# Graph attention kernel: a node group's x_l and x_r are loaded and bent four rounds ahead of its states

## The chip, the core and the metric

The kernel runs on one core of one Trainium2 chip. The metric is the device time of one execution in microseconds, compared as medians of runs of the two kernels on the same chip. Beside the times there is one profiled execution of the kernel, recorded instruction by instruction.

In a core, five sequencers run independently and meet at semaphores. TensorE (PE; its weight loads are listed as PEld) multiplies into PSUM. VectorE (DVE) and ScalarE (ACT) do elementwise work and reductions. GpSimd (POOL) issues the indirect gathers here. SyncE (SP) issues nearly all other DMAs, one after the other, in program order: a DMA whose condition isn't met holds up every DMA behind it.

## The reference

One layer of graph attention (GATv2, 8 heads of 16 channels) and a feed-forward block over 12,500 nodes and 400,000 edges that are sorted by destination:

```python
h  = relu(layernorm(x))
x_l, x_r = ln(h) @ W_l, ln(h) @ W_r                  # 12500 x 128
e  = edge_attr @ W_e                                 # self edges: the mean of edge_attr
m  = leaky_relu(x_l[src] + x_r[dst] + e, 0.2)
alpha = (m * att).sum(per head)
a  = softmax of alpha over the edges of each dst
out = segment_sum(x_l[src] * a, dst) + bias
h  = h + out
result = x + h + gelu(ln(h) @ W1 + b1) @ W2 + b2
```

Every node has a self edge, whose source and destination are the node itself.

## The kernel before

**Preparation.** The first part norms x, writes the x_l rows (136 floats: 128 and eight ones) to DRAM as `xl_dram`, and keeps h in SBUF (`h_sb`). x_r follows as three bf16 parts (`xs_dram`).

**Edges.** `window_edges` runs over 782 pairs of 256 edges, called c. It is a pipeline by hand: in round r, stage (late, f) of the table `stages` works on pair c = r - late. `gather` (-4) fetches the x_l rows of the pair's 512 edges with four indirect DMAs of 128 rows on GpSimd; in 24 pairs the rows are loaded from `late_dram` by SP in their place. `combine` (0) sums x_l, x_r and e in PSUM, `slope` and `bend` (1) make the leaky ReLU, `score` (2), `lowest` (3) and `weigh` (3) give the scores, their least and the exponents, `turn` (4), `keep_turned` (5) and `collect` (6) multiply by the gathered rows, `own_heads` (7) keeps what belongs to each head in the tile `rec`, and `put` (8) writes two records by SP to one of two DRAM tensors `state[0]` and `state[1]`, alternately. The buffer for gathered rows has 12 slots, so the gather of pair c needs the collecting of pair c - 12 to be done.

**Node groups.** The 98 tiles of 128 nodes are finished in 25 groups of 4 (the first has 2). A group has a round d["round"], from which the states of its nodes are complete in DRAM; groups are at least GAP = 23 rounds apart, and the last is at round 790, after the last `put` (round 789). The table `steps` gives each step's round after that: `f_load` (0) has SP load both states (`st`), x_l (`f_xl`) and x_r (`f_xr`), in this order; `f_order` (1, ACT) puts x_l in head order; `f_z` (2, PE) adds x_l and x_r; `f_bend` (3, ACT and DVE) makes the leaky ReLU of the self edges; `f_score` (4, PE) gives their scores; `f_low` (5, DVE) takes the least over both states and the self edge; then come `f_exp`, `f_den`, `f_out`, `f_h`, the second norm, the two products, gelu and `f_store` (19), which ends with SP's DMA of the output. The second gelu stands in its own table `early` at 17, which a round runs ahead of `stages`.

**What sets the order.** Everything here is scheduled by hand (`tc.manual_schedule`), so each engine's order is the order of this loop (L1320):

```python
for r in range(-AHEAD, max(last_round, groups[-1]["round"] + 20)):
    in_round(r, early)
    ...                          # stages: the edge pairs
    in_round(r, steps)           # the node groups
    ...                          # x_r of later nodes, late rows
    ...                          # late_stages: windows(r + 3), put(r - 8)
```

In a round SP therefore meets the loads of `steps` before the round's `put`. The states are read only when every earlier `put` to them has landed, and a later `put` waits for the load to be done. PSUM has two banks called acc, shared by `collect` and, through `bank_of`, by the group steps.

Of the kernel before, what the change touches and what calls it, by code (L numbers as in the profile page):

```python
# [47 lines left out]
AHEAD = 4  # L48
# [49 lines left out]
def node_groups(nt):  # L98

    first = nt % GN  # L100
    return ([(0, first)] if first else []) + [(t, GN) for t in range(first, nt, GN)]
# [6 lines left out]
def done_after(nt, n_edges):  # L108

    return [-(-(t + n) * P * edges_per_node(nt, n_edges) // U) + SPARE for t, n in node_groups(nt)]  # L110
# [24 lines left out]
def tile_gnn(  # L135
# [612 lines left out]
    with tc.If(fast == 1) as cmp:  # L748
        window_edges(
            tc, n_edges, ea_t, NT, NE, NUE, ident, ident_b, wer, we_z, negrep, diag, nid, farw, bias_r, b2_r, w1_sb, w2_sb,  # L750
            cols, xl_dram, xl_t, xs_dram, xs_t, dc_dram, du_dram, late_dram, state, clear, xr_steps, qs, raw_steps, raw, x_t, out_t, h_sb, src_sb, first_sb,
        )
# [74 lines left out]
def window_edges(  # L827
# [30 lines left out]
    with ExitStack() as es:  # L858
# [9 lines left out]
        NL = next(n for n in range(1, EQ + 1) if EQ % n == 0 and EQ // n <= 1024)  # L868
# [180 lines left out]
        groups = [{"t0": t, "n": n, "ts": slice(t, t + n)} for t, n in node_groups(NT)]  # L1049
# [5 lines left out]
        def bank_of(d, name, ring="acc"):  # L1055
            d[name] = ps2.tile([P, EPR], F32, name=ring)
            return d[name]

        def f_load(d):
            n, ts = d["n"], d["ts"]  # L1060
            d["st"] = fin.tile([P, 2, GN, SW], F32, name="st", tag="big", bufs=3)
            for i in range(2):
                nc.sync.dma_start(d["st"][:, i, 0:n], state[i].rearrange("(t p h) f -> p t (h f)", p=P, h=H)[:, ts, :])
            d["xl"] = fin.tile([P, GN, XW], F32, name="f_xl")
            nc.sync.dma_start(d["xl"][:, 0:n], xl_t[:, ts, :])
            d["xr"] = fin.tile([P, GN, NS, P], BF16, name="f_xr")
            nc.sync.dma_start(d["xr"][:, 0:n], xs_t[:, ts, :, :])
# [137 lines left out]
        def f_up(k):  # L1205
            def up(d):
                n, u = d["n"], bank_of(d, f"u{k}")
                nc.tensor.matmul(  # L1208
                    u[:, 0 : n * P],
                    w1_sb[:, k * P : (k + 1) * P],  # L1210
                    d["hT"][:, 0:n].rearrange("p t f -> p (t f)"),
                    start=True,
                    stop=True,
                )

            return up

        def f_gelu(k):
            def gelu(d):
                n = d["n"]  # L1220
                if k == 0:
                    d["gel"] = fin.tile([P, 2, GN * P], F32, name="gel", tag="big", bufs=3)
                nc.scalar.activation(
                    d["gel"][:, k, 0 : n * P], d[f"u{k}"][:, 0 : n * P], AF.Gelu, bias=cols[:, 5 + k : 6 + k]
                )

            return gelu
# [13 lines left out]
        def f_store(d):  # L1241
# [29 lines left out]
            (3, mean),  # L1271
        )
        SUM_STEP = 2
        early = ((17, f_gelu(1)),)
        steps = (
            (0, f_load),
            (1, f_order),
            (2, f_z),
            (3, f_bend),
            (4, f_score),  # L1280
            (5, f_low),
            (6, f_exp),
            (7, f_den),
            (8, f_out),
            (9, f_h),
            (10, f_stats),
            (11, f_root),
            (12, f_scale),
            (13, f_turn),
            (14, f_turned),  # L1290
            (15, f_up(0)),
            (16, f_up(1)),
            (16, f_gelu(0)),
            (18, f_down),
            (19, f_store),
        )
        GAP = 23
        last_round = n_pr + LATE + 2
        free = SUM_STEP * (NL - 1) + 5
        for d, u in zip(groups, done_after(NT, n_edges)):  # L1300
            d["round"] = max(free, (u // UP if u < NUE else n_pr) + LATE + 2)
            free = d["round"] + GAP

        def in_round(r, table, groups=groups):
            for k, f in table:
                for d in groups:
                    if d["round"] + k == r:
                        f(d)
# [8 lines left out]

        CLEAR = 8
        with tc.manual_schedule():
            for r in range(-AHEAD, max(last_round, groups[-1]["round"] + 20)):  # L1320
                in_round(r, early)
                for late, f in stages:
                    c = r - late
                    if 0 <= c < n_pr:
                        f(c)
                for late, f in sum_stages:
                    i, off = divmod(r - late, SUM_STEP)
                    if off == 0 and 0 <= i < NL:
                        f(i)
                if r > 0 and r % CLEAR == 0 and r // CLEAR < NT // GT:  # L1330
                    clear(r // CLEAR)
                in_round(r, steps)
                in_round(r, enumerate(xr_steps), qs[1:])
                in_round(r, enumerate(raw_steps), raw)
                for late, f in late_stages:
                    c = r - late
                    if 0 <= c < n_pr:
                        f(c)
# [358 lines left out]
```

## Time and profile before

| | |
|---|---|
| median of 3 runs | 4050.42 us (4048.72 to 4051.7) |
| the profiled execution's own time | 4055.89 us |
| its span, first to last instruction | 4053.7 us |
| mean granted TensorE clock | 0.955 |
| busy: PE / POOL / DVE / ACT | 3555.2 / 2984.9 / 2539.5 / 2135.2 us |
| chain of waits: PE / POOL / DMA / issue | 40% / 24% / 22% / 13% of the span |

The page of the profile has several views that are used below. The groups of instructions give, for each line, the count, the mean duration and the idle time of the engine ahead of them with its releaser. The view of one line gives its shortest, median and longest duration and its first and last start. The chain of waits follows the work that ended last back through what released each step. The timeline lists instructions in order of time; for SP it shows the issue of DMAs, not their landing.

The stages of the span in the profile: preparation until about 186 us, the edge pairs with the node groups among them from the first gather (186.4 us) until the last `own_heads` (ends at 4005.7 us), and the last node group alone, until 4053.7 us.

### The profile page before, as it was taken

How to read it: one execution, taken by the hardware profiler on the slowest of the kernel's cores; microseconds unless marked ns; L12 is line 12 of the kernel's file. 1: busy time of each engine (PE TensorE's matmuls, PEld its weight loads, DVE VectorE, ACT ScalarE, POOL GpSimd, SP SyncE). 2: the span in 40 equal slices, each digit the busy share in tenths (PEclk: the TensorE clock that was granted, in tenths of full speed). 3: DMA queues.
4: the chain of work that ended last, by engine and by line, in shares of the span. 5: the costliest groups of instructions: out<-in, count | busy, mean ns of one | idle time of the engine just before them, and what ended most of it. 6: DMA issues, size and time to landing. Idle time of an engine off the chain costs nothing.

```text
span 4053.7 us, 65778 instructions
## 1 busy us (share of the span) xinstructions
PE 3555.2 (88%) x19254; PEld 2501.5 (62%) x19255; DVE 2539.5 (63%) x5834; ACT 2135.2 (53%) x4638; POOL 2984.9 (74%) x3156
## 2 busy tenths in 40 slices
PE   2388888998989999999999999999989999989986
PEld 2356665665666666666666666666766666666664
DVE  5656665766666666666666666666666665666654
ACT  4544444544445555565455556555555555545543
POOL 4777777777777777777777777777777777777772
PEclk6699999999999999999999999999999999999998
DMA  5668878777766666656665665656666666565562
GB/s 160 198 165 198 185 194 197 171 163 165 172 124 126 126 124 131 123 121 129 132 125 124 128 129 120 136 123 117 124 136 126 124 130 128 107 135 114 120 134 50
DMA packets 648212, 560.85 MB, mean 138 GB/s; under 512 B 386387, under 2 KB 525506, under 8 KB 647602
## 3 DMA queue, kind: packets, MB, share of 16 engines
q1 hardware_dynamic: 547266, 339.01, 33.7%
q0 software_dynamic: 100000, 217.41, 30.2%
q8 instruction: 156, 2.56, 0.3%
q14 instruction: 214, 1.75, 0.2%
q10 hardware_dynamic: 576, 0.13, 0.0%
HBM read 489.81 MB, written 66.32 MB: 137 GB/s over the span
## 4 chain that ended last, share of the span: by engine, by line
PE 40%; POOL 24%; DMA 22%; issue 13%; SPq 1%; DVE 0%; ACT 0%; POOLq 0%; DVEq 0%; ACTq 0%
POOL xs L896 22%; DMA xs<-xl_dram,src_sb 21%; PE z L942 9%; PE acc L1000 8%; PE ab L960 7%; PE pt_ps L986 4%; PE z L938 4%; PE z L941 2%; PE ab L959 2%; POOL raw L270 2%; PE acc L1233 1%; PE acc L1208 1%; DMA lu<-in_dst 1%; SPq L282 0%; DMA state<-rec 0%
## 5 line engine op out<-in xcount | busy, mean ns | idle before, releaser
L896 POOL DMA_INDIRECT xs<-xl_dram,src_sb x3029 | 2873.0, 949 | 923.2 <-issue 796.0
L978 ACT ACTIVATE p<-ab,rec 128x256 f32<-128x256 f32 x1563 | 656.8, 472 | 1056.5 <-DVE rec L967 1044.3
L1009 DVE TENSOR_TENSOR own<-acc,diag 128x272 f32<-128x272 f32 x782 | 344.1, 440 | 1068.5 <-PE acc L1000 1039.6
L938 PE MATMUL z<-ident,xs 128*128 128x128 f32 x3125 | 573.3, 283 | 353.0 <-DMA xs<-xl_dram,src_sb 318.3
L938 PEld LDWEIGHTS z<-ident,xs 128*128 128x128 f32 x3125 | 399.5, 142 | 772.3 <-DMA xs<-xl_dram,src_sb 434.5
L1000 PE MATMUL acc<-xs,pt 128*128 128x136 f32 x6250 | 874.9, 284 | 0.2 <-DVE f_yo L1247 0.2
L942 PE MATMUL z<-ea,we_z 128*128 128x512 f32 x1564 | 835.4, 617 | 0.0
L1000 PEld LDWEIGHTS acc<-xs,pt 128*128 128x128 f32 x6250 | 802.6, 195 | 0.4 <-PE pt_ps L986 0.4
L960 PE MATMUL ab<-m,negrep 128*128 128x512 f32 x1564 | 801.4, 594 | 0.0
L991 ACT COPY pt<-pt_ps 128x512 f32<-128x512 f32 x782 | 455.9, 583 | 623.3 <-PE pt_ps L986 611.5
L986 PEld LDWEIGHTS pt_ps<-ident,p 128*128 128x128 f32 x3125 | 407.8, 146 | 438.2 <-issue 386.4
L967 DVE TENSOR_REDUCE rec<-ab 128x2 f32<-128x512 f32 x781 | 540.2, 692 | 123.4 <-PE ab L960 113.2
L953 DVE TENSOR_TENSOR m<-z,zs 128x512 f32<-128x512 f32 x782 | 533.0, 682 | 115.0 <-ACT zs L948 114.7
L948 ACT ACTIVATE zs<-z 128x512 f32<-128x512 f32 x782 | 472.2, 604 | 41.4 <-DMA dlw<-dc_dram 33.6
L986 PE MATMUL pt_ps<-ident,p 128*128 128x128 f32 x3125 | 489.2, 281 | 2.2 <-ACT pt L991 1.3
L1015 DVE TENSOR_REDUCE rec<-own 128x34 f32<-128x272 f32 x782 | 340.9, 436 | 26.7
L942 PEld LDWEIGHTS z<-ea,we_z 128*128 128x128 f32 x1564 | 306.5, 196 | 32.5
L960 PEld LDWEIGHTS ab<-m,negrep 128*128 128x128 f32 x1564 | 300.6, 192 | 37.1 <-issue 1.2
L941 PE MATMUL z<-ne,xrw 128*128 128x512 bf16 x782 | 304.0, 389 | 0.2 <-DMA xs<-xl_dram,src_sb 0.2
L959 PE MATMUL ab<-ne,farw 128*128 128x512 bf16 x782 | 299.6, 383 | 0.0
L924 DVE TENSOR_SCALAR ne<-dlw,nid 112x512 bf16<-112x512 bf16 x782 | 289.8, 371 | 13.0 <-DMA dlw<-du_dram 13.0
L270 POOL DMA_INDIRECT raw<-in_x,src_raw x96 | 95.5, 995 | 71.3 <-DMA raw_dram<-raw 40.1
(198 smaller groups left out, 2235.6 us busy)
## 6 DMA issues: line engine op xcount, KB each, us to landing
dlw<-dc_dram SPq DMA_DIRECT2D x196, 384.0 KB
ea<-in_ea_t SPq DMA_DIRECT2D x196, 256.0 KB
ea_s<-in_ea_t SPq DMA_DIRECT2D x98, 512.0 KB
xs<-xl_dram,src_sb POOLq DMA_INDIRECT x3029
state<-rec SPq DMA_DIRECT2D x1563, 9.0 KB
xrw<-xs_dram SPq DMA_DIRECT2D x782, 24.0 KB
state<-empty SPq DMA_DIRECT2D x28, 504.0 KB
st<-state SPq DMA_DIRECT2D x48, 288.0 KB
```

The lines of the kernel that those rows point to most:

```text
L896: nc.gpsimd.indirect_dma_start(out=xs[:, j, :], out_offset=None, in_=xl_dram, in_offset=bass.IndirectOffsetOnAxis(ap=src_sb[:, c * KP + j ...
L938: nc.tensor.matmul(z[:, j * P : (j + 1) * P], d["xs"][:, j, 0:P], ident, start=(j == 0), stop=False, is_transpose=True)
L941: nc.tensor.matmul(z[:, :e], xrw[c % NV], d["ne"][:, :e], start=False, stop=False)
L942: nc.tensor.matmul(z[:, :e], we_z[:, c % QP, :], d["ea"][:, :e], start=False, stop=True)
L948: nc.scalar.activation(d["zs"][:, :e], d["z"][:, :e], AF.Copy, scale=SLOPE)
L953: nc.vector.tensor_tensor(d["m"][:, :e], d["z"][:, :e], d["zs"][:, :e], op=OP.max)
L960: nc.tensor.matmul(ab[:, :e], negrep.rearrange("p n h -> p (n h)"), d["m"][:, :e], start=False, stop=True)
L967: nc.vector.tensor_reduce(d["rec"][:, :, CX], d["ab"].rearrange("p (u e) -> p u e", e=U), AX.X, OP.min)
L978: nc.scalar.activation(d["p"][:, us], d["ab"][:, us], AF.Exp, bias=d["rec"][:, i, CX:SH], scale=-1.0)
L986: nc.tensor.transpose(d["pt_ps"][:, js], d["p"][:, js], ident)
L991: nc.scalar.copy(d["pt"][:, :e], d["pt_ps"][:, :e])
L1000: nc.tensor.matmul(d["acc"][:, i, :], d["pt"][:, j * P : (j + 1) * P], d["xs"][:, j, :], start=(j == js[0]), stop=(j == js[-1]),)
```

## The change

`f_load` is cut in two. A new step `f_state` loads the two states; `f_load` keeps x_l and x_r. In the table, `f_load`, `f_order`, `f_z` and `f_bend` go to rounds -4, -3, -2 and -1, `f_state` takes round 0, and `f_score` and all that follow come three rounds earlier than they were (4 to 1, and so on to 19 to 16; the early gelu from 17 to 14). The first group may start at round 201 where it was 199; the loop's end follows the last step.

```diff
-        def f_load(d):
+        def f_state(d):
             n, ts = d["n"], d["ts"]
             d["st"] = fin.tile([P, 2, GN, SW], F32, name="st", tag="big", bufs=3)
             for i in range(2):
                 nc.sync.dma_start(d["st"][:, i, 0:n], state[i].rearrange("(t p h) f -> p t (h f)", p=P, h=H)[:, ts, :])
+
+        def f_load(d):
+            n, ts = d["n"], d["ts"]
             d["xl"] = fin.tile([P, GN, XW], F32, name="f_xl")
             nc.sync.dma_start(d["xl"][:, 0:n], xl_t[:, ts, :])
             d["xr"] = fin.tile([P, GN, NS, P], BF16, name="f_xr")
...
-        early = ((17, f_gelu(1)),)
+        early = ((14, f_gelu(1)),)
         steps = (
-            (0, f_load),
-            (1, f_order),
-            (2, f_z),
-            (3, f_bend),
-            (4, f_score),
-            (5, f_low),
...
-            (19, f_store),
+            (-4, f_load),
+            (-3, f_order),
+            (-2, f_z),
+            (-1, f_bend),
+            (0, f_state),
+            (1, f_score),
+            (2, f_low),
...
+            (16, f_store),
         )
         GAP = 23
         last_round = n_pr + LATE + 2
-        free = SUM_STEP * (NL - 1) + 5
+        free = SUM_STEP * (NL - 1) + 7
...
-            for r in range(-AHEAD, max(last_round, groups[-1]["round"] + 20)):
+            for r in range(-AHEAD, max(last_round, groups[-1]["round"] + 17)):
```

No instruction and no DMA is added or removed.

More of the change, by code (lines that the diff above doesn't have):

```diff
@@ L1273, in window_edges @@
         SUM_STEP = 2
-        early = ((17, f_gelu(1)),)
+        early = ((14, f_gelu(1)),)
         steps = (
-            (0, f_load),
-            (1, f_order),
-            (2, f_z),
-            (3, f_bend),
-            (4, f_score),
-            (5, f_low),
[L1282 to L1294, printed above, removed]
-            (19, f_store),
+            (-4, f_load),
[5 more added lines that the diff above has]
+            (2, f_low),
+            (3, f_exp),
+            (4, f_den),
+            (5, f_out),
+            (6, f_h),
+            (7, f_stats),
+            (8, f_root),
+            (9, f_scale),
+            (10, f_turn),
+            (11, f_turned),
+            (12, f_up(0)),
+            (13, f_up(1)),
+            (13, f_gelu(0)),
+            (15, f_down),
+            (16, f_store),
         )
```

## The prediction

> **What bounds the kernel now.** The first view is the page's groups of instructions, where the gather on GpSimd is the costliest, and then the view of that line.
>
> ```profile
> L896 POOL DMA_INDIRECT xs<-xl_dram,src_sb x3029 | 2873.0, 949 | 923.2 <-issue 796.0
> L896 POOL DMA_INDIRECT xs<-xl_dram,src_sb x3029: 940/945/1702, 186.4 to 3981.5; - x190
> ```
>
> Read the first and last start: 3029 gathers start between 186.38 and 3981.53 us, so one each 1.2533 us (3795.2 / 3028): 0.95 busy and 0.30 of issue, from first to last. The idle time is almost all "issue", so GpSimd's own sequence makes it. No gather waits for a buffer: if I pair the gather of c with the collecting of c - 12, whose slot it takes, GpSimd comes 17.7 us later than that in the median and 8.3 us in the nearest case (c = 109). TensorE idles for the gathered rows (434.5 us ahead of its weight loads in the views of waits). So until 3982.5 us, when the last gather ends, the clock is GpSimd's. Work of the other engines costs nothing there unless they fall back by over 8.3 us.
>
> The Trainium skill (Perfetto Trace Analysis, "Identifying the Most-Contended Engine") takes occupancy as the measure for GpSimd, and by it the bound would be TensorE: 88% against GpSimd's 74%. Then each stall that the new order gives or takes on TensorE in the 24 groups would count in full, about 24 us for one microsecond per group. The row says that GpSimd has no free time in its 74%, since the rest is issue. I take the row: the sum over the middle is zero.
>
> What follows the last gather is 71 us, and there the chain of waits, in order of time, decides:
>
> ```profile
> 3999.84 0.69 DVE f_yo L1247
> 4001.15 1.95 DMA state<-rec
> 4003.12 3.00 DMA state<-rec
> 4006.24 1.42 DMA state<-rec
> 4007.78 1.41 DMA state<-rec
> 4009.31 1.42 DMA state<-rec
> 4010.84 1.45 DMA state<-rec
> 4012.78 2.00 DMA state<-rec
> 4015.24 0.50 SPq L1063
> 4015.79 4.96 DMA f_xl<-xl_dram
> 4020.89 1.08 PE acc L1081 x4
> 4021.99 1.48 PE acc L1086 x12
> 4023.49 0.70 ACT f_zs L1095
> 4024.21 0.76 DVE f_m L1097
> 4025.02 1.89 PE acc L1103 x8
> ```
>
> Columns: start, length, what. Group 23 (round 764) stores at round 783. SP waits there for f_yo until 4000.5 us, and the last 13 puts stand behind it. They then go one pair per landing, 1.53 us apart, although their records were ready by 4005.7. The last lands at 4014.78; only then are the states loaded, and behind them x_l, which lands after 4.96 us, then z, its bend and the scores. Timeline rows of the same stretch:
>
> ```profile
> 4000.56 0.39 SPq L1248 DMA_DIRECT2D out<-f_yo  x1
> 4001.15 11.96 SPq L1022 DMA_DIRECT2D state<-rec  x13
> 4014.79 0.95 SPq L1063 DMA_DIRECT2D st<-state  x2
> 4026.93 0.19 DVE L1114 TENSOR_TENSOR f_mn<-f_mn,acc 128x32 f32<-128x32 f32 x1 [1.85 <-PE acc L1103]
> ```
>
> From the states' issue at 4014.79 (call it T) to the first minimum that needs states and scores, 12.14 us pass; from there to the span's end 26.77 us.
>
> **The change, part by part.**
>
> *x_l, x_r, order, z and bend out of the last group's chain.* Its `f_load` goes to round 786, `f_z` to 788, right behind the last collecting (787); they lie beside the last puts. Loads at about 4002.2 (below), landed by 4007 or so; z 2.6 us, f_zs 0.7, f_m 0.8, scores 1.9 by the rows above: 4013 to 4014, while the states can't have landed. So the chain is T, states landed, two minima. The states' landing isn't on the page. From above, x_l lands at T + 5.96 with both states ahead of it; from below, the earliest put in the middle that follows two state loads issues 3.41 us after the first. In one group its second put waits, and the row shows it:
>
> ```profile
> 1275.26 0.95 SPq L1063 DMA_DIRECT2D st<-state  x2
> 1278.76 1.88 SPq L1022 DMA_DIRECT2D state<-rec  x2
> ```
>
> A pair of puts takes 0.9 us undisturbed, so this second one came at 1280.3, 5.0 us after the first load's issue. I take T + 4.9, plus one minimum (0.20) and gaps: the second minimum at T + 5.15. **Gain 7.0 us (5.9 to 8.4).** Nothing replaces it as last: the scores are about 3 us early.
>
> *Later steps three rounds earlier.* Group 23's `f_store` moves from round 783 to 780. TensorE is busy without a break from 3951.5 on, and the steps that pass round 780 were already behind that point, so its work up to the last collecting is the same: one f_up (0.86) and f_down (1.8) come ahead of pair 780, 2.6 us, and are missing behind it. What goes are stalls in the shortened last rounds (0.66 us for the gelu on ACT, 0.2 to 0.4 for f_yo). I work the last rounds out with the row durations (round 3.95; turning 0.44, collecting 0.93, score 1.14): the last `own_heads` ends near 4004.1, and c = 777 is ready at 3999.8. SP now has its wait for f_yo near 3990.7, and its puts, a pair each 1.5 us against rounds of 2.5 to 4, have caught up at 777, issued at 4000.8.
>
> *What SP's queue gets in exchange.* Round 786 puts x_l and x_r, 272 + 384 KB, ahead of the last four puts (778 to 781). The Trainium skill (DMA: Bandwidth & Descriptors, "Queues, rings and completion order") speaks against this: each DMA engine consumes a ring's descriptors in order, so the puts get behind 656 KB; at that page's 435 GB/s ceiling an estimated 1.5 us. The rows give more: behind the output's 256 KB the second pair took 3.00 us, not 1.42. By size this is 1.58 x 656 / 256 = 4.0 us extra; nothing is the other end. With the page T would be about 4011.6, with the full 4.0 near 4014. I take 2.6 us extra, between, since the loads are issued ahead of the first such pair and part of them has gone before it. So: loads at 4001.7 and 4002.3, put 778 at 4003.0, landed 4007.0; 779 at 4008.5, 780 at 4010.1, 781 issued 4010.6 and landed 4012.6. **T = 4012.6, gain 2.2 us (0.3 to 4.6).** The low end is T = 4014.5, the high one T = 4010.2, without any delay.
>
> *The cover of the state load shrinks.* `f_low` stood five rounds behind it and now stands two. On DVE the queue behind a late `f_low` is the next round's `own_heads`, `lowest` and `bend`, for which TensorE waits, and then the gathers' slots. Two rounds after the load stands `f_z` in the trace of before; it begins 9.65 to 23.9 us after the first state load in the 24 groups, against a landing of about 5.0. In the tightest group 4.6 us are left: cost nothing. Without that cover, each microsecond would first eat the 8.3 us of slot margin.
>
> *Other moves, one answer for all.* f_x's load (one 256 KB DMA at `f_h`), the output DMA and the two ACT table loads per group keep their order among themselves; `f_x` is read ten rounds later as before. The shared buffers f_b, f_c and f_d keep several rounds between last reader and next writer (output DMA at 16, x_l in order at 19), and z has three rounds to the scores in place of two in the acc banks. `free` + 2 delays groups 0 to 19 by up to two rounds, under GpSimd's clock: nothing.
>
> **Sum.** 7.0 + 2.2 = 9.2 us (6.2 to 13.0) off the span of 4053.7, so 4044.5, and off the execution's own 4055.89, so 4046.7. That execution is 5.5 us above the median of runs; from the median, 4050.42 - 9.2 = **4041.2 us**. Of a median here some 0.2%, 8.1 us, can be told from no change, so the forecast stands close to that bound.
>
> **The rivals.**
>
> - *The puts give the gain back.* The loads ahead of them delay the last put to where it was, or the stalls near the end are only moved. For it: 3.00 us behind a smaller DMA. Against: the wait for f_yo goes. Left is 7.0 us or somewhat less: 4043.5 to 4044, within 0.2%. Chance 0.28.
> - *The puts run free.* 656 KB of loads don't hold 72-byte rows back; T = 4010.2: 4.6 + 7.0 = 11.6, so 4038.8. For it: the first pair behind the output took 1.95 us. Chance 0.17.
> - *The states become the new wait, slower than before.* `f_low` at two rounds stops DVE in each of the 24 groups. It decides from a landing 9.65 + 8.3, about 18 us, after issue; at 19.5 us GpSimd would lose 1.5 us 24 times, 36 - 9 = 27 us: 4077. For it: SP's waits for puts reach 5.0 us, and one put follows the state loads only after 9.37. Against: all others are at 3.4 to 6.5. Chance 0.06.
> - *It doesn't shorten the end*, because the scores or z wait behind something on PE: z at 788 is the last thing in its queue, so only late x_l rows could do it. It is inside the first rival.
>
> **How the numbers follow.** Forecast 0.49, rivals 0.28, 0.17 and 0.06. The range reaches from the free puts with a faster state landing (4037) to the first rival with the low end of the state's gain and 2 us of measurement (4047). Of the forecast's own share about a tenth falls short of 8.1 us: faster 0.61, same 0.33, slower 0.06.
>
> **What would show it.** Right: gathers still 1.2533 us apart, the last starting near 3981.5; f_yo of group 23 near 3990; the states' issue at 4010 to 4014; the second minimum about 5 us later, waiting for a DMA and not for PE; nearly the same 26.8 us after it. Wrong: gaps between gathers, or DVE waiting at L1113 in the middle (the third rival); T at 4014 or later (the first); z or the scores behind the states.

## The result, and the profile after

| | before | after |
|---|---|---|
| median of 11 runs each | 4050.42 us (4047.63 to 4053.25) | 4040.26 us (4038.02 to 4044.95) |
| ratio after / before, 95% interval | | 0.9976 [0.9968, 0.9984] |
| span of the profiled execution | 4053.7 us | 4041.3 us |

The change takes 10.2 us, 0.25%, off the median; the interval, 6.5 to 13.0 us, lies wholly below the kernel before. In a later set of runs, with before at 4057.23 us, the changed kernel gave 0.9978 [0.9969, 0.9987].

The chain of waits of the changed kernel, in order of time, where the last group begins (start, length, what):

```profile
3999.57 4.69 DMA f_xr<-xs_dram
4004.31 1.47 PE acc L1089 x12
4005.81 0.70 ACT f_zs L1098
4006.53 0.45 DVE f_m L1100
4006.99 1.42 DMA state<-rec
4008.53 1.43 DMA state<-rec
4009.97 0.40 SPq L1063
4010.41 3.73 DMA st<-state
4014.23 0.22 DVE f_mn L1116
4014.55 0.20 DVE f_mn L1117
```

x_r, z and the bend now stand ahead of the last puts. The step from `f_m` to a put is the view's inference and isn't a wait of the program: a put needs only its `rec`, and the last reduction into `rec` ends at 4002.49. In the changed kernel's second profile two puts are issued before the bend is over, the second at 4004.68:

```profile
4004.14 1.88 SPq L1022 DMA_DIRECT2D state<-rec  x3
4004.52 0.75 DVE L1100 SCALAR_TENSOR_TENSOR f_m<-acc,el,f_zs 128x512 f32<-128x512 f32 x1 [5.53 <-ACT f_zs L1098]
```

Behind the states' issue at 4009.97 there is only their landing and the first minimum; the second, which needs the scores too, starts 4.58 us after the issue, where 12.14 us passed before. The issues of DMAs by SP in the same stretch, from the timeline (start, length, queue, line, what):

```profile
3988.74 0.39 SPq L1251 DMA_DIRECT2D out<-f_yo  x1
...
3999.09 0.43 SPq L1068 DMA_DIRECT2D f_xl<-xl_dram  x1
3999.57 0.50 SPq L1070 DMA_DIRECT2D f_xr<-xs_dram  x1
4000.33 0.93 SPq L1022 DMA_DIRECT2D state<-rec  x2
4004.55 0.33 SPq L1022 DMA_DIRECT2D state<-rec  x1
...
4009.97 0.95 SPq L1063 DMA_DIRECT2D st<-state  x2
```

SP leaves its wait for f_yo at 3988.7 us, not at 4000.5, and by 3999 the puts have caught up. The pair at 4000.33 has 656 KB of loads ahead of it; the next put can go only at 4004.55, 4.2 us later, where an undisturbed pair lands in 1.4. By the chain, f_xr itself lands at 4004.26 (3999.57 + 4.69): the puts follow right behind it.

In the middle, the gathers have the same form (count, shortest, median and longest ns, first and last start):

```profile
L896 POOL DMA_INDIRECT xs<-xl_dram,src_sb x3029: 940/945/1568, 186.0 to 3979.9; - x190
```

That is (3979.9 - 186.0) / 3028 = 1.2529 us for each, before 1.2533.

A table by stage compares the two profiles and serves for the experiments too. "Last gather" is the start of the last gather; T is SP's first issue for the last group's states.

| profiled run | last gather | T after it | second minimum after T | end after that | span |
|---|---|---|---|---|---|
| before | 3981.5 | 33.3 | 12.14 | 26.8 | 4053.7 |
| after | 3979.9 | 30.1 | 4.58 | 26.8 | 4041.3 |
| last group alone | 3978.4 | 34.7 | 4.52 | 27.9 | 4045.5 |
| first 24 groups alone | 3978.3 | 27.1 | 11.46 | 26.5 | 4043.4 |
| front steps alone | 3977.1 | 36.3 | 4.47 | 27.4 | 4045.3 |
| loads ten rounds ahead | 3978.6 | 25.9 | 4.46 | 26.8 | 4035.8 |
| states two rounds later | 3979.5 | 29.9 | 4.57 | 26.8 | 4040.8 |
| z six times | 3978.3 | 31.4 | 4.56 | 26.8 | 4041.1 |
| output later | 3979.2 | 28.0 | 4.49 | 26.9 | 4038.6 |
| loads early, output later | 3977.7 | 27.4 | 4.56 | 26.6 | 4036.3 |

The 12.4 us between the first two spans are 1.6 of earlier gathers, 3.2 of T and 7.6 behind T. The first is the difference of two executions, as the last section shows. The 7.6 are the change: every profile with the last group changed has 4.46 to 4.70 there. The 3.2 of T are less sure, from one profile of before. Executions with the changed kernel's own end have T at 29.9, 30.1, 30.5 and 31.4. In the profile of before the granted clock of TensorE was 0.66 from 3950 to 3955 us, in the changed one 1.00; by an estimate from these figures (0.34 of 5 us) that is up to 1.7 us of T. The profile with 31.4 had such a stretch too (0.83 from 3950 to 3960).

### The profile page after: what moved, and what is told of

Same layout as the page of the kernel before. It is cut to its first block, busy times and chain, and to the rows that moved or that the text cites. A ratio compares the mean times of both kernels' runs of the same rounds, so it can differ in the third digit from the quotient of the medians.

```text
span 4041.3 us, 65594 instructions
## 1 busy us (share of the span) xinstructions
PE 3542.6 (88%) x19060; PEld 2500.8 (62%) x19255; DVE 2538.2 (63%) x5834; ACT 2135.4 (53%) x4638; POOL 2983.6 (74%) x3156
## 4 chain that ended last, share of the span: by engine, by line
PE 37%; POOL 25%; DMA 23%; issue 14%; SPq 1%; DVE 0%; ACT 0%; POOLq 0%; DVEq 0%; ACTq 0%
POOL xs L896 23%; DMA xs<-xl_dram,src_sb 21%; PE z L942 8%; PE acc L1000 8%; PE ab L960 7%; PE z L938 4%; PE pt_ps L986 4%; PE z L941 2%; POOL raw L270 2%; PE ab L959 1%; PE acc L1211 1%; PE acc L1236 1%; DMA lu<-in_dst 1%; SPq L282 0%; DMA state<-rec 0%
## 5 line engine op out<-in xcount | busy, mean ns | idle before, releaser
L1000 PE MATMUL acc<-xs,pt 128*128 128x136 f32 x6250 | 878.0, 285 | 0.0
L1000 PEld LDWEIGHTS acc<-xs,pt 128*128 128x128 f32 x6250 | 805.9, 196 | 0.0
L941 PE MATMUL z<-ne,xrw 128*128 128x512 bf16 (+1 forms) x781 | 302.0, 387 | 0.2 <-DMA ea_s<-in_ea_t 0.2
L959 PE MATMUL ab<-ne,farw 128*128 128x512 bf16 x589 | 225.4, 383 | 2.9 <-ACT p L978 2.9
```

Source lines behind the costliest of these rows:

```text
L941: nc.tensor.matmul(z[:, :e], xrw[c % NV], d["ne"][:, :e], start=False, stop=False)
L1000: nc.tensor.matmul(d["acc"][:, i, :], d["pt"][:, j * P : (j + 1) * P], d["xs"][:, j, :], start=(j == js[0]), stop=(j == js[-1]),)
```

## The experiments

**Which groups the gain comes from.** Two runs split the groups: one gives the new steps to the last group alone, the other to all but the last. `old_steps` is the table of before with `f_state` and `f_load` both at 0.

```diff
-                in_round(r, early)
+                in_round(r, early, groups[-1:])
+                in_round(r, old_early, groups[:-1])
...
-                in_round(r, steps)
+                in_round(r, steps, groups[-1:])
+                in_round(r, old_steps, groups[:-1])
```

(The second run has `groups[:-1]` and `groups[-1:]` exchanged, and the loop's end at 20 for 17.)

> Only the last of the 25 groups gets the new order; the other 24 keep the old steps, so group 23 still stores in round 783. Theory (the gain has two parts, both in the end behind the last gather): x_l, z and the bend leave the last chain, 7.6 us, but the puts still stand behind group 23's f_yo and now get 656 KB of loads among them, so the states are issued some 3 us later than before: about 4046, 4 to 5 us under the kernel before. If instead all of the gain came from the last group's own chain, the changed kernel's time, about 4040; if it came from the 24 groups, no change, 4050.

> The first 24 groups get the new order, the last keeps the old one (loads of states, x_l and x_r at its round, then order, z, bend, scores). Theory: group 23 stores in round 780, SP's puts are not held and no loads stand among them, so the states are issued near 4006 to 4008; the old 12.1 us from there to the minimum stay: about 4043, 7 to 8 us under the kernel before. If the gain came from the last group's chain alone: 4050.

Measured: last group alone 4048.39 us, 0.9991 [0.9982, 1.0] of before's 4051.74; all but the last 4044.74 us, 0.9982 [0.9973, 0.9991]. So 3.4 and 7.0 us, together 10.4, against 10.2 for the whole change. The interval of the first reaches no change, and both are some 3.6 us wide to each side: that the sum fits so well is chance. SP's issues with the last group alone:

```profile
3996.57 0.39 SPq L1251 DMA_DIRECT2D out<-f_yo  x1
3997.16 4.66 SPq L1022 DMA_DIRECT2D state<-rec  x6
4001.86 0.43 SPq L1068 DMA_DIRECT2D f_xl<-xl_dram  x1
...
4003.09 8.86 SPq L1022 DMA_DIRECT2D state<-rec  x7
4013.07 0.95 SPq L1063 DMA_DIRECT2D st<-state  x2
```

The puts are held by f_yo as before, and now have the loads among them as well: T comes 34.7 us after the last gather, 1.4 later than before. The chain behind T is short (4.52 us), and that leaves a small gain, less than the 4 to 5 us expected. With all but the last group changed, SP's issues and the second minimum:

```profile
3988.10 0.39 SPq L1251 DMA_DIRECT2D out<-f_yo  x1
3988.70 15.59 SPq L1022 DMA_DIRECT2D state<-rec  x19
4005.40 0.96 SPq L1063 DMA_DIRECT2D st<-state  x2
...
4016.86 0.19 DVE L1117 TENSOR_TENSOR f_mn<-f_mn,acc 128x32 f32<-128x32 f32 x1 [1.85 <-PE acc L1106]
```

All 19 last puts go without loads among them, and T comes 27.1 us after the last gather, the 6 us that group 23's earlier store is worth by itself. But the minimum waits for TensorE again, 11.5 us behind T. The rows show both parts, the time alone only the second clear of noise; neither run gives the whole.

**The front steps alone.** Loads, order, z and bend ahead for every group; scores and all later steps at 4 to 19 as before.

```diff
             (0, f_state),
-            (1, f_score),
-            (2, f_low),
+            (4, f_score),
+            (5, f_low),
...
-            (16, f_store),
+            (19, f_store),
```

> All groups: x_l and x_r are loaded, ordered, added and bent four rounds ahead, but the scores and all later steps stay where they were (4 to 19). Theory: as with the last group alone, since what the other groups do in the middle is under the clock of the gathers: about 4046. If the groups in the middle count, it differs from that run by more than 3 us.

Measured 4047.49 us, 0.9991 [0.9982, 1.0]. It agrees with the last group alone within 1 us, although here 24 more groups have their front steps moved: moving them in the middle is worth nothing that the medians can tell.

**What sets the clock of the middle.** The changed kernel, with z made six and twenty times over in 23 groups; each time starts the bank anew, so only the last counts.

```diff
+            for _ in range(1 if d["t0"] >= groups[-2]["t0"] else 6):
-            for i in range(n):
+                for i in range(n):
...
```

> The changed kernel, with the sum z of x_l and x_r done six times over in each of 23 groups (all but the last two), the result of the last being used: 5 x 1.1 us more TensorE work per group, some 127 us in all. If GpSimd's gathers set the clock of the middle: nothing, the changed kernel's time within 3 us. If TensorE, the engine with the largest share of busy time, bounds it: 4040 + 127 = about 4167, or at least half of that.

> As the run with z done six times, but twenty times in each of the 23 groups: 19 x 1.1 = 20.9 us more TensorE work per group. Theory: 23 rounds of gathers take 23 x 5.01 x 31/32 = 111.7 us, TensorE's own work for them some 98 us, so it has about 13 us per group to spare and the gathers' buffers another 8 once; 5.5 us more fitted, 20.9 don't: some 7 us times 20 groups, 100 to 250 us more than the changed kernel, with gaps between the gathers for the first time. If GpSimd's clock held whatever TensorE does: no change.

Measured: six times 4041.3 us, 0.9975 [0.9965, 0.9985], against 0.9976 for the changed kernel; twenty times 4225.19 us, 1.0429 [1.0384, 1.0474], 185 us more than the changed kernel by its first median. The idle time of GpSimd ahead of a gather (what ended it: us in total, times), first with six, then with twenty:

```profile
its engine sat idle before it (us, times) until:
  issue: 778.0, 2552
  DMA xs<-xl_dram,src_sb: 53.9, 177
  PE pt_ps L986: 25.3, 83
...
```

```profile
its engine sat idle before it (us, times) until:
  issue: 780.1, 2558
  PE acc L1000: 201.6, 82
  DMA xs<-xl_dram,src_sb: 45.1, 148
...
```

With six there is nothing in it but the 0.3 us between gathers, whatever releaser the view names. With twenty, 82 gathers wait for the collecting (L1000), which frees their slots, 201.6 us in all, and the kernel is longer by about as much. One z takes 1.27 us in the middle and six take 6.84, so some 125 us of added work on the busiest engine cost nothing, and about 475 us broke through: GpSimd sets the clock with a reserve on TensorE between these sizes, as the sum of spare time (13 us per group) had it. The busy time of PE grew by less than was added (from 3542.6 us to 3618.9 and 3906.7), while the mean granted clock went from 0.956 to 0.965 and 0.974; a part of the reserve may lie there.

The rival is TensorE with its 88%, which would have put most of the added work into the time. The prediction read this out of the Trainium skill (Perfetto Trace Analysis, "Identifying the Most-Contended Engine"), but for TensorE that section sets the matmul's busy share aside and takes the share of the weight loads, beside the arithmetic done. The page of before has both:

```profile
PE 3555.2 (88%) x19254; PEld 2501.5 (62%) x19255; DVE 2539.5 (63%) x5834; ACT 2135.2 (53%) x4638; POOL 2984.9 (74%) x3156
```

By weight loads TensorE (62%) stands behind GpSimd (74%), and section and runs agree on the engine. What occupancy doesn't show is that GpSimd's 74% leave it nothing to spare.

**Does the state load need its cover?** The changed kernel with `f_state` at 2, in front of `f_low` in the same round. (In the changed kernel itself the nearest `f_low` of the 24 groups begins 7.54 us after the load's first issue.)

> The changed kernel with the states' load in the same round as f_low, which needs them (round 2 instead of 0). Theory: VectorE now waits for the landing, up to some 5 us in a part of the groups, but this is less than the 8.3 us by which the gathers' buffers are free ahead of time, and the last group's rounds are empty: the changed kernel's time within 2 us. If the wait takes the place of the hidden load: 24 groups times 2 to 5 us, 50 to 100 us more.

Measured 4041.16 us, 0.9976 [0.9967, 0.9985]. VectorE does wait for the landing now (us in total, times, longest):

```profile
DVE f_mn L1116 <- DMA st<-state: 30.8, 10, 6.9
```

6.9 of it is the last group's wait, which the changed kernel has too; the other 23.9 us in 9 groups are new, and none of them is in the time. They stay under the 8.3 us of reserve that the gathers' slots have. This is the mechanism of the slower rival, made on purpose: it exists, and at this size it is free.

**The loads among the last puts.** The changed kernel with `f_load` at -10 for -4; then with the output's DMA as a step of its own, two rounds behind the additions; then both.

```diff
-            (-4, f_load),
+            (-10, f_load),
...
+            (18, f_out_store),
```

> The changed kernel with x_l and x_r loaded ten rounds ahead instead of four, so that the last group's 656 KB stand ahead of SP's wait for f_yo and not among the last puts. Theory: in the changed kernel these loads held put 778 for 4.2 us instead of 1.4, so the states are issued about 3 us earlier and as early as in the run with only the first 24 groups changed (27 us after the last gather): about 4037, 3 us under the changed kernel. If the loads don't delay the puts: the changed kernel's time, 4040 to 4041.

> The changed kernel with the output's DMA two rounds behind the additions that make it, so that SP never waits for f_yo. Theory: SP's waits for f_yo (226 us over 20 groups) lie in the middle under the gathers' clock, and by round 786 the puts have caught up anyway: the changed kernel's time within 1.5 us, 4039 to 4042. If SP's holding counts in the middle: over 10 us less.

> Both: loads ten rounds ahead and the output's DMA two rounds later. Theory: as the early loads alone, about 4037, at most 1 us less.

Measured: loads early 4037.61 us, 0.9966 [0.9952, 0.9979]; output later 4041.52, 0.9974 [0.9964, 0.9985]; both 4039.74, 0.9971 [0.9959, 0.9983]. SP's issues with the loads early:

```profile
3973.81 0.41 SPq L1068 DMA_DIRECT2D f_xl<-xl_dram  x1
...
3985.66 0.39 SPq L1251 DMA_DIRECT2D out<-f_yo  x1
3986.29 17.10 SPq L1022 DMA_DIRECT2D state<-rec  x19
4004.51 0.95 SPq L1063 DMA_DIRECT2D st<-state  x2
```

The loads are out before SP waits, and T comes 25.9 us after the last gather for 30.1. In this profile that is 4.2 us; with the output later as well it is only 0.6 (27.4 for 28.0), and the time of both, expected at 4037, is above that of the loads alone. The output's DMA as a step of its own doesn't end SP's waits for f_yo but shortens them, as the changed kernel and then this run show (us in total, times, longest):

```profile
SPq L1251 <- DVE f_yo L1250: 226.6, 20, 24.6
SPq L1253 <- DVE f_yo L1250: 69.7, 20, 24.7
```

The longest is the last group's in both. Some 157 us fewer of these waits in the middle are worth nothing: the time is that of the changed kernel.

Since the difference in time is near what can be measured, the changed kernel and the early loads ran again side by side, with one more version: group 23's steps from turning to the output held back to rounds 785 to 791 (two more tables, and `f_store` writing to the buffer f_a).

```diff
+        held_steps = (
+            (21, f_turn),
+            (22, f_turned),
+            (23, f_up(0)),
+            (23, f_up(1)),
+            (24, f_gelu(0)),
+            (24, f_gelu(1)),
+            (25, f_down),
+            (27, f_store),
+        )
```

> The changed kernel once more, on the same chip as the two others of this call: 4040 to 4041.

> The run with the loads ten rounds ahead once more, on the same chip: 3 us under the changed kernel if the delay of the puts behind the loads is real, and no difference if the first comparison was chance.

> The early loads, and for group 23 alone the steps from turning to the output (the products, the gelus, the store) held back from rounds 774 to 780 to rounds 785 to 791, where TensorE has next to no edge work. Theory: from some 30 us before the last gather's end TensorE has no gap, so its 3.95 us for these steps and the gelu's waits stand in the path to the last put; without them the edge rounds end earlier until they meet the landing of the last gathered rows, some 1.5 to 3 us: about 4035 to 4036. If the last rows or the puts bound this stretch already: the time of the early loads, within 1 us.

Measured, with before at 4057.23 us on that chip, so that the expected 4040 to 4041 does not hold and the ratio does: changed kernel 4048.72, 0.9978 [0.9969, 0.9987]; loads early 4047.65, 0.9976 [0.9965, 0.9986]; held back 4045.34, 0.9966 [0.9952, 0.9979]. The three intervals overlap, so the 3 us of the early loads are not confirmed by time: 1.1 us here, 2.7 between the first medians of two separate comparisons. The profiles agree with one another better: T comes 27.2 us after the last gather with early loads and 30.5 without, much as in the first pair of profiles (25.9 and 30.1). Holding back gives 27.6 in its profile, no gain over the early loads; there, the last put took 3.1 us to land. Whether it helps stays open.

## Why the prediction was right

Forecast 4041.2 us, measured 4040.26, by the steps that were forecast. That the two agree within 1 us is luck in part: the interval of the gain is 6.5 to 13.0 us, the profiles give 10.8 behind the last gather where 9.2 was forecast, and some sizes below were off.

- *The middle is GpSimd's, so its sum is zero.* Right, and shown: front steps in 24 groups, 125 us of TensorE work, 24 us of waits on VectorE and 157 us of SP's waits for f_yo all leave the time where it was. The page's rule that the prediction set against this was misread, as said with that experiment.
- *z and bend leave the last chain.* Forecast 7.0 us (T + 5.15 to the second minimum), measured 7.6 (T + 4.58): the first minimum begins 4.26 us after T, where the states' landing was put at 4.9. The 4.9 came from a put in a middle group, which is only an upper bound. That x_l and x_r no longer stand behind them is hardly the reason: by the DMA packets in the traces the last of the states ends 3.73 us after T in before, with both behind it, and 3.50 in the changed kernel. A size, within its bounds. The second minimum follows the first one, and waits for no TensorE result, as forecast; the stretch behind it is 26.75 us against 26.77.
- *Group 23's earlier store frees SP.* f_yo was forecast for 3990.7 and ended at 3988.7; the puts had caught up before the loads, which SP issued at 3999.1 and not at 4001.7. Of this, 1.6 us is the profile's earlier gathers.
- *The loads hold the last puts.* Forecast: the first pair behind them lands after 4.0 us; measured 4.2. This was the step on which the row (1.58 us extra behind 256 KB) and the page's bandwidth (an estimated 1.5 us for 656 KB) differed: 2.8 us extra for that pair is near the 2.6 taken. But the next pair took 2.4 us where 1.5 was forecast, so the loads go with some 3.6 us extra, near the 4.0 by size; why the second is slow was not tried. In the other profiles with this end the first pair takes 4.2 to 5.7 us and the second 1.6 or 2.5. The last put took 1.44 us, where 2.5 with the gap ahead of it were forecast: so the way from the first of these puts to T came out at 9.64 us for 9.6 by errors that made up for one another. The ring order that the Trainium skill states (DMA: Bandwidth & Descriptors, "Queues, rings and completion order") agrees with it; its bandwidth alone was too small a price.
- *T.* Forecast 2.2 us earlier; measured 3.2 relative to the last gather, 4.8 in the profile's own time. The bounds of 0.3 to 4.6 hold the first and not the second; up to 1.7 us of either may be the clock's, as said under the table.
- *The state load's cover.* No VectorE wait for the states in the 24 groups of the changed kernel; its one wait, 7.0 us, is the last group's. The cover is thinner than forecast: the nearest `f_low` comes 7.54 us after the load, where `f_z` in the trace of before stood for it with 9.65.

The rivals: the puts did not give all back and did not run free; "free" is what the early loads give. The slower rival needs a landing some 18 us behind the issue, and the run with the load in the same round shows waits that stay below that.

## What to carry to other kernels

A pipeline has one clock in the middle and a chain at its end, and a schedule change is priced in each apart: here the front steps, moved by four rounds, were worth nothing measurable in 24 groups and several us in the last. Look for the engine whose instructions follow each other without a wait, even if its busy share isn't the largest, and add work to its neighbour to see how much reserve there is. When a load is moved ahead, look at what then stands behind it in its queue: the first pair of the small writes that end the chain landed 2.8 us later for two loads that nobody waited for.

## What was not expected

The kernel's time drifts with the period of the gathers, by as much as the change is worth. In the profiles it lies between 1.2513 us (the changed kernel's second profile, 187.7 to 3976.6) and 1.2547 us (the held-back version, 186.7 to 3986.0); over 3028 periods that is 10.4 us. Two rows, in this order:

```profile
L896 POOL DMA_INDIRECT xs<-xl_dram,src_sb x3029: 940/944/1594, 187.7 to 3976.6; - x190
...
L896 POOL DMA_INDIRECT xs<-xl_dram,src_sb x3029: 941/947/1589, 186.7 to 3986.0; - x190
```

The median of one gather differs by 3 ns, which over 3029 gathers is 9 of the 10.4 us. What makes this difference wasn't tried. It also appears between the profiles of one comparison, so the comparisons that count here are medians against the kernel before on the same chip, and stretches measured from the last gather.
